# Filling TensorE's gaps in a graph attention layer: an earlier turn, a value product moved, rows normalised ahead

## The chip, the core and the metric

The kernel runs on one core of one Trainium2 chip. The metric is the device time of one execution in microseconds (us); lower is better. Before the change the median of three executions is 959.8 us (958.86 to 959.97).

A core has five engines that run side by side and wait for each other through semaphores. TensorE (PE) multiplies matrices and also transposes them, by a product with an identity; its results go to an accumulator memory called PSUM. VectorE (DVE), ScalarE (ACT) and GpSimd (POOL) do the elementwise work, and SyncE (SP) mostly issues DMA transfers between the device memory and the on-chip buffers. Every engine takes its own instructions in the order that was laid down when the kernel was built. That order is worked out by a scheduler from an estimate of durations; it follows the program as it is written where several instructions could go, but an instruction that the estimate holds to be ready may be put into a gap ahead of its place in the program.

## The reference

Two layers over the same 4096 nodes with 512 features, and one dense 4096 x 4096 matrix `adj`. Cut to what matters:

```python
# layer 0: attention inside each of 32 graphs of 128 nodes; b and edge_encoding are both adj
h = relu(layernorm(x))
query, key, value = h @ Wq.T + bq, h @ Wk.T + bk, h @ Wv.T + bv
a = where(mask, query @ key.T / sqrt(512), 0)
scores = (a + adj + adj) * where(mask, 1, -1e6)      # mask: same graph
x = x + (softmax(scores) * mask) @ value
# layer 1: 8 heads of 64; the attention's logits are s_i + t_j where adj > 0
h = relu(layernorm(x))
mx = einsum('nf,hfd->hnd', h, W)
attn = softmax(where(adj > 0, s_i + t_j, -inf))
x = x + concat_heads(attn @ mx)
```

In layer 0 only the 128 x 128 blocks on the diagonal enter the attention, but every entry of `adj` enters the softmax's sum. In layer 1 the term s_i is the same in a whole row and falls out of the softmax, so the kernel needs exp(t_j) only, and a 0/1 mask made of `adj`.

## The kernel before

The 4096 rows are 32 tiles of 128, and layer 0 takes two tiles (a pair, `G = 2`) at a time: 16 pairs. Query and key weights are multiplied together once ("fold"), so that scores are `(h M + c) h^T`. The products are in 32-bit floats.

First come the helpers that the change touches. `norm` is the layer norm: statistics on VectorE, the inverse root on GpSimd, the scaling on VectorE. `relu_T` turns a tile with four transpositions on TensorE and copies it out of PSUM on ScalarE, with the relu in the copy:

```python
    def norm(src, hn, of=None):
        mean, rstd = of or moments(src)
        nc.vector.tensor_scalar(hn, src, mean, rstd, ALU.subtract, ALU.mult)

    def relu_T(ps_pool, hn, dst):
        pt = ps_pool.tile([P, KC, P], F32, name="pt")
        for k in range(KC):
            nc.tensor.transpose(pt[:, k, :], hn[:, ts(k, P)], ident)
        nc.scalar.activation(dst, pt, AF.Relu)
```

The fold, cut to its product, which is made in four quarters `m`:

```python
    def fold(sb, tmp, work, ps_t, ps_p):
        wkT_sb = load_weight(tmp, wkT, "wkT_sb", KC, tag="lo")
        wqT_sb = load_weight(tmp, wqT, "wqT_sb", KC, tag="lo")
        # ... both turned back (L195), the biases' terms (L209) ...
        for m in range(KC):
            if m == 2:
                # ... u_sb and z_sb, the biases' terms spread over the partitions
            pp = ps_p.tile([P, D], F32, name="pp")
            for k in range(KC):
                nc.tensor.matmul(                                              # L231
                    pp, wq[:, k, ts(m, P)], wk[:, k, :], start=(k == 0), stop=(k == KC - 1)
                )
            nc.scalar.mul(m_sb[:, m, :], pp, SCALE)
        return m_sb, c_sb, u_sb, z_sb
```

Layer 0's parts for a pair, and for a row tile of layer 1 that is prepared while layer 0 still runs:

```python
            def normed1(i):                          # layer 1, row tile i
                row = sb2.tile([P, D], F32, name="row1")     # two buffers
                nc.sync.dma_start(row, x1_d[i])              # L392
                norm(row, row)
                hT = sb2.tile([P, KC, P], F32, name="hT1")
                relu_T(ps_t, row, hT)
                return hT

                def normed(g):
                    hT = sb.tile([P, KC, G * P], F32, name="hT")
                    r = sb.tile([P, G], F32, name="r", bufs=3)
                    hns = []
                    for t in range(G):
                        hn = sb.tile([P, D], F32, name="hn")  # two buffers
                        norm(xg[g][:, t, :], hn)
                        relu_T(ps_t, hn, hT[:, :, ts(t, P)])
                        hns.append(hn)
                    for t, hn in enumerate(hns):
                        # ... r = relu(hn) . u_sb + z_sb, on VectorE (L433) and GpSimd
                    return hT, r
```

`queries` is 16 matmuls for a pair (L445) with four copies on ScalarE to `gT` (L449); `values` is four products for a tile (L457) and an addition on VectorE; `scores` multiplies `gT` and `hT` (L503), adds twice the diagonal block of `adj` and takes the exponential on ScalarE; `turned` transposes the exponentials (L522) and has ScalarE copy them to `sT`; `attend` multiplies `sT` with the values (L530), adds the input on VectorE and stores the row as `x1_d`. `read` goes over the pair's rows of `adj`: VectorE makes the mask bytes of layer 1, and ScalarE takes the exponential of all entries for the sum (L480, `junk`), and the next loads of `adj` are issued.

The head and the loop over pairs:

```python
                m_sb, c_sb, u_sb, z_sb = fold(wp, lo, sb, ps_t, ps_p)
                load_pair(0)
                wv = load_weight(wp, wvT, "wv")
                # ... bv, seven loads of adj, load_pair(1) ...
                hT, r = normed(0)
                vs = [values(hT, t) for t in range(G)]
                # ... look: read of pair 0 ...
                gT = queries(hT)
                nhT, nr = normed(1)
                for g in range(NG):
                    # ... load_pair(g + 2) ...
                    def prepare_on(now):
                        if now:
                            i = len(ahead)
                            ahead.append(normed1(i))
                            if i:
                                prepare(i - 1, ahead[i - 1], part_tile(lo, i - 1))

                    s = scores(g, hT, gT, r, *look)
                    prepare_on(last)
                    if not last:
                        ngT = queries(nhT)
                    sT = turned(s)
                    prepare_on(3 <= g and g % 2)
                    nvs = []
                    for t in range(G):
                        look_on(t)                    # read of the next pair
                        attend(sT, vs[t], g, t)
                        prepare_on(last and t == 0)
                        if not last:
                            nvs.append(values(nhT, t))
                    # ... the next pair takes over ...
                    if g + 2 < NG:
                        nhT, nr = normed(g + 2)
```

`prepare` is layer 1's projection of one row tile (L259, 16 matmuls) with its exponentials. After the loop the remaining row tiles of layer 1 are prepared, and then the mask is multiplied with the prepared rows (L308), row tile by row tile.

Of the kernel before, what the change touches and what calls it, by code (L numbers as in the profile page):

```python
# [20 lines left out]
P = 128  # L21
# [32 lines left out]
def kernel(  # L54
# [53 lines left out]
    def load_adj(pool, k):  # L108

        a = pool.tile([P, NH], F32, name="a")  # L110
        nc.sync.dma_start(a, adj[ts(k // 2, P), ts(k % 2, NH)])
        return a
# [14 lines left out]
# [4 lines that stand above are left out]
# [19 lines left out]
    def load_weight(pool, src, name, pieces=1, **kw):  # L150
        t = pool.tile([P, KC, D], F32, name=name, **kw)
        n = KC // pieces
        for k in range(0, KC, n):
            nc.sync.dma_start(
                t[:, k : k + n], src[k * P : (k + n) * P].rearrange("(k p) m -> p k m", p=P)
            )
        return t
# [12 lines left out]
            )  # L170
        return w

    def fold(sb, tmp, work, ps_t, ps_p):


        wkT_sb = load_weight(tmp, wkT, "wkT_sb", KC, tag="lo")
        wqT_sb = load_weight(tmp, wqT, "wqT_sb", KC, tag="lo")
        def spread_bias(b):
            pp = ps_p.tile([P, D], F32, name="pp")
            for k in range(KC):  # L180
                nc.tensor.matmul(
                    pp[:, ts(k, P)], b[:, k : k + 1].to_broadcast([P, P]), ident,
                    start=True, stop=True,
                )
            row = work.tile([P, D], F32, name="b_row", tag="hn")
            nc.scalar.copy(row, pp)
            return row

        nat = []
        for n, wT in enumerate((wkT_sb, wqT_sb)):  # L190
            w = tmp.tile([P, KC, D], F32, name=f"w{n}", tag="lo")
            for k in range(KC):
                pt = ps_t.tile([P, KC, P], F32, name="pt")
                for m in range(KC):
                    nc.tensor.transpose(pt[:, m, :], wT[:, k, ts(m, P)], ident)  # L195
                nc.scalar.copy(w[:, :, ts(k, P)], pt)
                if n == 0 and k == 0:
                    rows = [spread_bias(b) for b in (bk_sb, bq_sb)]
            nat.append(w)
        wk, wq = nat  # L200
        m_sb = sb.tile([P, KC, D], F32, name="m_sb")
        c_sb = sb.tile([P, KC], F32, name="c_sb")
        u_col = sb.tile([P, KC], F32, name="u_col")
        u_sb = sb.tile([P, D], F32, name="u_sb")
        z_sb = sb.tile([P, 1], F32, name="z_sb")
        for dst, wT, row in ((u_col, wqT_sb, rows[0]), (c_sb, wkT_sb, rows[1])):
            for k in range(KC):
                wb = work.tile([P, D], BF16, name="wb", tag="hu", bufs=1)
                nc.vector.scalar_tensor_tensor(  # L209
                    wb, wT[:, k, :], SCALE, row, ALU.mult, ALU.mult, accum_out=dst[:, k : k + 1]  # L210
                )
        zk = sb.tile([P, KC], F32, name="zk")
        zp = sb.tile([P, 1], F32, name="zp")
        nc.vector.scalar_tensor_tensor(
            zk, bq_sb, SCALE, bk_sb, ALU.mult, ALU.mult, accum_out=zp
# [6 lines that stand above are left out]
                        pp[:, ts(k, P)], u_col[:, k : k + 1].to_broadcast([P, P]), ident,  # L222
                        start=True, stop=True,
                    )
                nc.scalar.copy(u_sb, pp)
                pp = ps_p.tile([P, D], F32, name="pp")
                nc.tensor.matmul(pp[:, :1], zp.to_broadcast([P, P]), one, start=True, stop=True)
                nc.scalar.copy(z_sb, pp[:, :1])
            pp = ps_p.tile([P, D], F32, name="pp")
            for k in range(KC):  # L230
                nc.tensor.matmul(  # L231
# [4 lines that stand above are left out]
# [136 lines left out]
    with ExitStack() as straight:  # L372
# [4 lines left out]
        with ExitStack() as prep:  # L377
# [9 lines left out]

            two = []

            def normed1(i):  # L390
                row = sb2.tile([P, D], F32, name="row1")
                nc.sync.dma_start(row, x1_d[i])  # L392
                norm(row, row)
                hT = sb2.tile([P, KC, P], F32, name="hT1")
                relu_T(ps_t, row, hT)
                return hT
# [17 lines left out]
            with (  # L414
# [2 lines left out]
                tc.tile_pool(name="sb0", bufs=2, side="right") as sb,  # L417
                tc.tile_pool(name="ps_s0", bufs=1, space=PSUM) as ps_s,
            ):
                def normed(g):  # L420


                    hT = sb.tile([P, KC, G * P], F32, name="hT")
                    r = sb.tile([P, G], F32, name="r", bufs=3)
                    hns = []
                    for t in range(G):
                        hn = sb.tile([P, D], F32, name="hn")
                        norm(xg[g][:, t, :], hn)
                        relu_T(ps_t, hn, hT[:, :, ts(t, P)])
                        hns.append(hn)  # L430
                    for t, hn in enumerate(hns):
                        hu = sb.tile([P, D], BF16, name="hu", bufs=1)
                        nc.vector.scalar_tensor_tensor(  # L433
                            hu, hn, 0.0, u_sb, ALU.max, ALU.mult, accum_out=r[:, t : t + 1]
                        )
                    nc.gpsimd.tensor_scalar(r, r, z_sb, None, ALU.add)
                    return hT, r

                def queries(hT):

# [96 lines left out]
                def load_pair(g):  # L537
                    xg[g] = sb.tile([P, G, D], F32, name="xg", bufs=3)
                    nc.sync.dma_start(
                        xg[g], x[g * G * P : (g + 1) * G * P, :].rearrange("(t p) d -> p t d", p=P)  # L540
                    )

                NG = NT // G
                xg, aa = {}, {}
                m_sb, c_sb, u_sb, z_sb = fold(wp, lo, sb, ps_t, ps_p)
                load_pair(0)
                wv = load_weight(wp, wvT, "wv")
                nc.scalar.dma_start(bv_sb, bv.to_broadcast([P, D]))
                for k in range(4):
                    aa[k] = load_adj(ap, k)  # L550
                load_pair(1)
                for k in range(4, AB):
                    aa[k] = load_adj(ap, k)
                hT, r = normed(0)
                vs = [values(hT, t) for t in range(G)]
                look = seen()
                for t in range(G):
                    look[2].append(read(t, look[0][:, t, :], look[1][t]))
                gT = queries(hT)
                nhT, nr = normed(1)  # L560
                ahead = []
                for g in range(NG):
                    last = g + 1 == NG
                    if g + 2 < NG:
                        load_pair(g + 2)
                    if g == 1:
                        w1x = load_w1(pool1, sb)
                    nlook = seen()

                    def look_on(t):  # L570
                        if not last:
                            i = G * (g + 1) + t
                            nlook[2].append(read(i, nlook[0][:, t, :], nlook[1][t]))

                    def prepare_on(now):
                        if now:
                            i = len(ahead)
                            ahead.append(normed1(i))
                            if i:
                                prepare(i - 1, ahead[i - 1], part_tile(lo, i - 1))  # L580

                    s = scores(g, hT, gT, r, *look)
                    prepare_on(last)
                    if not last:
                        ngT = queries(nhT)
                    sT = turned(s)
                    prepare_on(3 <= g and g % 2)
                    nvs = []
                    for t in range(G):
                        look_on(t)  # L590
                        attend(sT, vs[t], g, t)
                        prepare_on(last and t == 0)
                        if not last:
                            nvs.append(values(nhT, t))
                    if not last:
                        hT, r, gT, vs, look = nhT, nr, ngT, nvs, nlook
                    if g + 2 < NG:
                        nhT, nr = normed(g + 2)

# [477 lines left out]
```

## Time and profile before

| | before |
|---|---|
| median time | 959.8 us |
| span of the profiled execution | 956.0 us |
| TensorE busy / weight loads busy | 934.7 us / 810.8 us |
| VectorE busy | 465.0 us |
| ScalarE busy | 267.9 us |
| GpSimd busy | 179.9 us |
| aggregate products of layer 1 (L308, two groups) | 247.4 and 237.3 us |
| projection of layer 1 (L259) | 117.0 us |
| value products (L457) | 116.4 us |
| query products (L445) | 113.2 us |
| bytes moved by DMA | 156.63 MB, mean 164 GB/s |

All lines of the profile are of one profiled execution. A timeline row gives the start in us from the span's start, the duration in us, the engine, the line of the kernel, the operation with what it writes and reads, how many instructions are merged in the row, and in brackets how long the engine was idle before it and what ended that. "PE" is TensorE's matmuls and transpositions, "PEld" its weight loads, which overlap with them. The times of matmuls in the timeline overlap a little with their neighbours, because matmuls are pipelined and their ends are modelled; the chain of waits counts each only until the next begins. "MATMUL pt" are transpositions of rows, "pp" products.

Layer 0 fills the first 350 us or so, with TensorE, VectorE, ScalarE and the DMA engines all at work; the rest of layer 1's rows is prepared until about 460 us; from there to the end the aggregate products run one after another.

### The profile page before, as it was taken

The numbers are of one execution on the slowest core, as the hardware profiler recorded it, in microseconds if no ns is written. First come the engines' busy times: TensorE is split into PE (matmuls) and PEld (weight loads), VectorE is DVE, ScalarE is ACT, GpSimd is POOL, SyncE is SP. The second block draws the span as 40 slices with busy tenths as digits, with TensorE's granted clock in tenths as the row PEclk, the third lists the DMA queues.
The fourth block names the chain that finished last, engine by engine and source line by source line (L and its number), as shares of the span: only waits on it lengthen the run. The fifth ranks groups of instructions, "written<-read, shape, count | busy, mean of one in ns | idle before, by whom it ended". The sixth has DMA issues, their size and how long they took to land.

```text
span 956.0 us, 13142 instructions
## 1 busy us (share of the span) xinstructions
PE 934.7 (98%) x4987; PEld 810.8 (85%) x4987; DVE 465.0 (49%) x992; ACT 267.9 (28%) x539; POOL 179.9 (19%) x344
## 2 busy tenths in 40 slices
PE   8999999999999999999999999999999999999997
PEld 5676667776666777778999999999999999999997
DVE  4678877775775445674445242423324242423322
ACT  5776576666662224532000000000000000000000
POOL 2311213211211224655210100101010110101010
PEclk9999999999999999999999999999999999999999
DMA  9989889998985213575131312122231313222111
GB/s 343 417 344 390 332 312 364 348 367 322 367 349 199 78 34 110 165 198 133 56 85 49 88 50 84 51 82 72 61 89 45 89 50 83 57 77 85 48 45 36
DMA packets 61062, 156.63 MB, mean 164 GB/s; under 512 B 6722, under 2 KB 23490, under 8 KB 52290
## 3 DMA queue, kind: packets, MB, share of 16 engines
q1 hardware_dynamic: 51058, 138.70, 42.0%
q10 hardware_dynamic: 9936, 17.05, 4.8%
q8 instruction: 40, 0.66, 0.3%
q14 instruction: 28, 0.23, 0.1%
HBM read 117.97 MB, written 37.75 MB: 163 GB/s over the span
## 4 chain that ended last, share of the span: by engine, by line
PE 86%; DVE 4%; DMA 4%; ACT 3%; issue 1%; POOL 1%; SPq 0%; ACTq 0%; DVEq 0%
PE pg L308 50%; PE pp L457 12%; PE pp L445 10%; PE pp L259 5%; PE pp L530 3%; PE pss L503 3%; PE pt L136 1%; DMA row<-x_d 1%; DVE stats L118 1%; DMA a<-adj 1%; PE pl L308 1%; DVE blocks L623 1%; ACT rowm L698 1%; POOL rstd L124 1%; DMA mw<-a_d 1%
## 5 line engine op out<-in xcount | busy, mean ns | idle before, releaser
L308 PE MATMUL pg<-part,ata 128*128 128x348 f32 x1536 | 247.4, 322 | 0.6 <-DVE e L268 0.6
L308 PEld LDWEIGHTS pg<-part,ata 128*128 128x128 f32 x1536 | 245.0, 188 | 1.0 <-issue 1.0
L308 PE MATMUL pg<-part,atb 128*128 128x348 f32 x1472 | 237.3, 322 | 0.0
L308 PEld LDWEIGHTS pg<-part,atb 128*128 128x128 f32 x1472 | 235.0, 188 | 0.1
L321 ACT COPY tot<-pg 128x522 f32<-128x522 f32 x31 | 18.6, 599 | 455.9 <-PE pg L308 455.9
L480 ACT ACTIVATE junk<-a 128x2048 bf16<-128x2048 f32 (+15 forms) x92 | 124.5, 1353 | 49.9 <-DVE x L532 28.0
L259 PE MATMUL pp<-w1x,hT 128*128 128x256 f32 (+1 forms) x512 | 117.0, 384 | 2.0 <-DVE e L268 1.8
L457 PE MATMUL pp<-wv,hT 128*128 128x512 f32 x256 | 116.4, 598 | 0.0
L445 PE MATMUL pp<-hT,m_sb 128*128 128x256 f32 x512 | 113.2, 379 | 0.0
L259 PEld LDWEIGHTS pp<-w1x,hT 128*128 128x128 f32 x512 | 95.3, 190 | 19.3 <-issue 4.7
L296 DVE CAST atb<-at 128x4096 fp32r<-128x4096 fp8e4 x16 | 36.7, 2293 | 153.1 <-PE pg L308 153.1
L445 PEld LDWEIGHTS pp<-hT,m_sb 128*128 128x128 f32 x512 | 96.2, 190 | 12.8 <-issue 0.5
L296 DVE CAST ata<-at 128x4096 fp32r<-128x4096 fp8e4 (+1 forms) x17 | 37.3, 2196 | 141.8 <-PE pg L308 141.8
L457 PEld LDWEIGHTS pp<-wv,hT 128*128 128x128 f32 x256 | 49.2, 192 | 61.8 <-issue 61.8
L146 DVE TENSOR_SCALAR a<-a 128x512 fp8e4<-128x512 f32 x256 | 98.8, 466 | 1.6 <-DMA a_d<-a 1.4
L733 POOL COPY den_all<-tot 128x1 f32<-128x1 f32 x31 | 5.7, 184 | 367.9 <-DVE tot L322 355.9
L737 POOL TENSOR_TENSOR tot<-tot,row 128x512 f32<-128x512 f32 x31 | 39.9, 1286 | 61.9 <-DVE tot L327 57.8
L122 POOL TENSOR_SCALAR ve<-mv 128x1 f32<-128x1 f32 x64 | 16.3, 258 | 163.3 <-DVE mv L120 163.3
L243 POOL TENSOR_TENSOR part<-e,part 128x522 fp32r<-128x522 f32 x32 | 42.8, 1336 | 18.5 <-ACT part L240 18.4
L287 DVE STREAM_TRANSPOSE at<-mw 128x1024 f32<-128x1024 f32 x32 | 39.6, 1238 | 5.3 <-DMA mw<-a_d 5.3
L124 POOL TENSOR_TENSOR rstd<-ve,neghalf 128x1 f32<-128x1 f32 x64 | 38.5, 604 | 4.6
L461 DVE TENSOR_TENSOR v<-pp,bv_sb 128x512 f32<-128x512 f32 x32 | 22.0, 689 | 32.2 <-PE pp L457 32.2
(113 smaller groups left out, 691.0 us busy)
## 6 DMA issues: line engine op xcount, KB each, us to landing
a<-adj SPq DMA_DIRECT2D x64, 1024.0 KB, 12.8
a_d<-a SPq DMA_DIRECT2D x32, 512.0 KB, 10.1
mw<-a_d SPq DMA_DIRECT2D x128, 128.0 KB, 4.0
row<-x_d SPq DMA_DIRECT2D x41, 256.0 KB, 3.5
xg<-x SPq DMA_DIRECT2D x16, 512.0 KB, 4.6
x_d<-x ACTq DMA_DIRECT2D x32, 256.0 KB, 4.2
out<-tot ACTq DMA_DIRECT2D x31, 256.0 KB, 3.7
rowm<-x_d SPq DMA_DIRECT2D x16, 256.0 KB, 4.8
```

The costliest lines, as they stand in the source:

```text
L124: nc.gpsimd.tensor_tensor(rstd, ve, neghalf, ALU.pow)
L146: nc.vector.tensor_scalar(a8v[:, u], av[:, u], 0.0, None, ALU.is_gt, saturate=False)
L243: nc.gpsimd.tensor_sub(dst[:, :, 1, :], e3, dst[:, :, 0, :].bitcast(F32))
L259: nc.tensor.matmul(pm[g][:, :n], hT[:, k, :], w1x[:, k, g * HW : g * HW + n], start=(k == 0), stop=(k == KC - 1),)
L287: nc.vector.transpose(at8.rearrange("p c n b -> p (c n b)").bitcast(F32).rearrange("p (c u n) -> p c u n", c=NW, n=B), mw.rearrange("p u ( ...
L296: nc.vector.tensor_copy(at[:, c0 * BY : c1 * BY].rearrange("p (c b) q -> p c b q", b=BY), at8[:, c0:c1].rearrange("p c q b -> p c b q"),)
L308: nc.tensor.matmul(pg[:, : 2 * CW1], at[:, j, :], part(j)[:, c].rearrange("p s w -> p (s w)"), start=(j == 0), stop=(j == NT - 1),)
L445: nc.tensor.matmul(pp[:, : G * P], m_sb[:, k, ts(m, P)], hT[:, k, :], start=(k == 0), stop=(k == KC - 1),)
L457: nc.tensor.matmul(pp, hT[:, k, ts(t, P)], wv[:, k, :], start=(k == 0), stop=(k == KC - 1))
L480: nc.scalar.activation(junk[:, c0:c1], a[:, c0:c1], AF.Exp, scale=2.0 * NEG, accum_out=sums[:, n : n + 1],)
L503: nc.tensor.matmul(pss[:, t, :], gT[:, k, ts(t, P)], hT[:, k, ts(t, P)], start=(k == 0), stop=(k == KC - 1),)
L737: nc.gpsimd.tensor_add(num, num, row)
```

## The change

There are three parts. None changes what is computed.

- Pair 0 is turned within the fold, ahead of the last quarter of the weights' product, by a function that the fold calls at `m == 3`. For this `normed` is cut in two: `turned0` normalises and turns, `row_terms` makes `r`. The loads that used to follow the fold in the program are handed to it too and are written right after its own. The aim is that the value product of pair 0 finds its turned rows ready when the fold ends.
- In the loop, the next pair's first value product comes between the turned exponentials and the first attention instead of after it, so that the copy of `sT` has a product to hide behind.
- `normed1` is cut in two: `begin1` loads and normalises a row tile of layer 1, `turned1` turns it. A row is begun one turn ahead of the turn in which it is transposed (a turn is an odd pair from 3 on, and three times in the last pair), with its first load moved to pair 2, so that its transpositions have no load or normalisation to wait for.

The diff, with blank lines and unchanged stretches cut:

```diff
-    def fold(sb, tmp, work, ps_t, ps_p):
+    def fold(sb, tmp, work, ps_t, ps_p, loads, first):
         wkT_sb = load_weight(tmp, wkT, "wkT_sb", KC, tag="lo")
         wqT_sb = load_weight(tmp, wqT, "wqT_sb", KC, tag="lo")
+        loads()
@@ in the four quarters of the product
+            if m == 3:
+                first()
             pp = ps_p.tile([P, D], F32, name="pp")
@@
-            def normed1(i):
+            rows1 = []
+
+            def begin1():
                 row = sb2.tile([P, D], F32, name="row1")
-                nc.sync.dma_start(row, x1_d[i])
+                nc.sync.dma_start(row, x1_d[len(rows1)])
                 norm(row, row)
+                rows1.append(row)
+
+            def turned1(row):
                 hT = sb2.tile([P, KC, P], F32, name="hT1")
                 relu_T(ps_t, row, hT)
                 return hT
@@
-                def normed(g):
+                def turned0(g):
                     hT = sb.tile([P, KC, G * P], F32, name="hT")
-                    r = sb.tile([P, G], F32, name="r", bufs=3)
                     ...
+                    return hT, hns
+
+                def row_terms(hns):
+                    r = sb.tile([P, G], F32, name="r", bufs=3)
                     for t, hn in enumerate(hns):
                         ...
-                    return hT, r
+                    return r
@@
-                m_sb, c_sb, u_sb, z_sb = fold(wp, lo, sb, ps_t, ps_p)
-                load_pair(0)
-                wv = load_weight(wp, wvT, "wv")
-                ... (bv, adj, load_pair(1): the same lines)
-                hT, r = normed(0)
+                first = []
+
+                def loads():
+                    load_pair(0)
+                    first.append(load_weight(wp, wvT, "wv"))
+                    ... (bv, adj, load_pair(1): the same lines)
+
+                m_sb, c_sb, u_sb, z_sb = fold(
+                    wp, lo, sb, ps_t, ps_p, loads, lambda: first.extend(turned0(0))
+                )
+                wv, hT, hns = first
+                r = row_terms(hns)
@@
-                nhT, nr = normed(1)
+                nhT, hns = turned0(1)
+                nr = row_terms(hns)
@@ in the loop over pairs
-                            ahead.append(normed1(i))
+                            ahead.append(turned1(rows1[i]))
@@
                     prepare_on(last)
+                    if last:
+                        begin1()
                     if not last:
                         ngT = queries(nhT)
                     sT = turned(s)
                     prepare_on(3 <= g and g % 2)
+
+                    for _ in range({2: 1, NG - 2: 1, NG - 1: 0}.get(g, int(3 <= g and g % 2))):
+                        begin1()
                     nvs = []
                     for t in range(G):
                         look_on(t)
+                        if not last and t == 0:
+                            nvs.append(values(nhT, t))
                         attend(sT, vs[t], g, t)
                         prepare_on(last and t == 0)
-                        if not last:
+                        if not last and t:
                             nvs.append(values(nhT, t))
@@
-                        nhT, nr = normed(g + 2)
+                        nhT, hns = turned0(g + 2)
+                        nr = row_terms(hns)
```

More of the change, by code (lines that the diff above doesn't have):

```diff
@@ L544 @@
                 xg, aa = {}, {}
-                m_sb, c_sb, u_sb, z_sb = fold(wp, lo, sb, ps_t, ps_p)
-                load_pair(0)
-                wv = load_weight(wp, wvT, "wv")
[L548 to L553, printed above, removed]
-                hT, r = normed(0)
+                first = []
+                def loads():
+                    load_pair(0)
+                    first.append(load_weight(wp, wvT, "wv"))
+                    nc.scalar.dma_start(bv_sb, bv.to_broadcast([P, D]))
+                    for k in range(4):
+                        aa[k] = load_adj(ap, k)
+                    load_pair(1)
+                    for k in range(4, AB):
+                        aa[k] = load_adj(ap, k)
+                m_sb, c_sb, u_sb, z_sb = fold(
[3 more added lines that the diff above has]
+                r = row_terms(hns)
                 vs = [values(hT, t) for t in range(G)]
```

## The prediction, made before the changed kernel was run

> **What bounds the kernel now.** I read the page first, then the list of what TensorE waited for, then the timeline of TensorE alone through layer 0, and last the timelines of ScalarE and of the DMA issues around its three largest holes. The page's first part says which engine to look at:
>
> ```profile
> PE 934.7 (98%) x4987; PEld 810.8 (85%) x4987; DVE 465.0 (49%) x992; ACT 267.9 (28%) x539; POOL 179.9 (19%) x344
> ```
>
> TensorE is busy for 934.7 of 956.0 us. The change removes no matmul, so all it can return is idle TensorE time (21.3 us) and time in which matmuls run slower than they could. The wait list says how much of that has a cause with a name (columns: us in total, times, longest us):
>
> ```profile
> PE pt L195 <- DMA wkT_sb<-wkT: 3.8, 1, 3.8
> PE pt L136 <- DVE row L130: 2.6, 1, 2.6
> PE pp L530 <- ACT sT L524: 2.4, 4, 1.4
> PE pt L136 <- DVE hn L130: 2.0, 1, 2.0
> ```
>
> The first is the start of the program. The other three, 7.0 us together, are what the three parts aim at. The timeline shows each (start, duration, engine, what; in brackets the idle time before). First the head, TensorE and ScalarE:
>
> ```profile
> 27.22 1.04 PE L136 MATMUL pt<-ident,hn 128*128 128x128 f32 x8
> ...
> 28.38 1.08 ACT L137 ACTIVATE hT<-pt 128x512 f32<-128x512 f32 x2
> ...
> 30.27 0.33 PE L136 MATMUL pt<-ident,hn 128*128 128x128 f32 x1 [2.02 <-DVE hn L130]
> ...
> 30.44 7.04 PE L457 MATMUL pp<-wv,hT 128*128 128x512 f32 x16
> ```
>
> Pair 0 is turned at 27.22, after the whole weights' product. Its copy to hT ends only at 29.46, and one transposition of pair 1 has been put in the queue before the values, and waits for VectorE. TensorE idles from about 28.25 to 30.27. Next, pair 2 (L522 turns the exponentials, L530 is the attention):
>
> ```profile
> 91.63 0.38 PE L522 MATMUL pss<-ident,s 128*128 128x128 f32 x2
> 93.36 1.12 PE L530 MATMUL pp<-v,sT 128*128 128x512 f32 x2 [1.35 <-ACT sT L524]
> 94.32 3.60 PE L457 MATMUL pp<-wv,hT 128*128 128x512 f32 x8
> ```
>
> Attention needs sT, which ScalarE copies out of PSUM; the copy stood behind a 1.15 us and a 0.84 us exponential of the adjacency. The value product just after it (3.43 us in the chain) needs nothing of this. Last, pair 8:
>
> ```profile
> 213.31 1.04 PE L136 MATMUL pt<-ident,hn 128*128 128x128 f32 x8
> 216.95 0.44 PE L136 MATMUL pt<-ident,row 128*128 128x128 f32 x2 [2.60 <-DVE row L130]
> 217.22 1.34 PE L530 MATMUL pp<-v,sT 128*128 128x512 f32 x2
> 218.36 5.02 PE L457 MATMUL pp<-wv,hT 128*128 128x512 f32 x8
> ```
>
> A transposition of a layer 1 row waits for VectorE, and the value product after it takes 5.02 instead of 3.60 us. The chain of waits over this stretch names the row's DMA as the root, and the table by windows shows the clock that was granted (before the last two numbers):
>
> ```profile
> 203.59 10.84 DMA row<-x_d
> ...
> 214.45 0.70 DVE stats L118
> ```
>
> ```profile
> 210.00:220.00 10.00, 7.40 (x32) 5.01 (x31) 6.69 (x22) 6.70 (x13) 1.37 (x4) 0.89 1.02 423
> ```
>
> The row was issued at 203.59, in the middle of a burst of adjacency loads that starts when the old pair's input comes free (201.07), and landed 10.84 us later.
>
> **What the Trainium skill says.** "TensorE: Matmul & The Clock Gate", Part 1 (The HAM clock gate), says that about 3.4 us without work halves the clock and that the window runs freely. The trace agrees in part: after the hole at 213 to 217 the mean clock was 0.89, while after the shorter hole at 28 to 30 it stayed at 1.00. The same page, in its paragraph on engine queue depths, says that ScalarE and VectorE queues are strictly first in, first out; here ScalarE ran the last gT copy and then sT at 216.12 only after an exponential that had waited until 213.86 for its DMA, which agrees. "DMA: Bandwidth & Descriptors", Issuing engines are not separate DMA queues, lets one expect a small load to share the same 16 engines with the large ones; the row's 10.84 us beside a median of 4.8 us for its line agrees.
>
> **The change, part by part.** I take the distance from one pair's scores to the next pair's in the chain of waits, and compare it with the sum of the parts when nothing waits: scores 1.79, queries 6.91, turning the exponentials 0.22, attention twice 0.86, values twice 3.43, turning the next pair 0.87: 18.37 us. A pair that also prepares a layer 1 row has 3.51 for the projection and 0.43 for four transpositions: 22.31.
>
> Measured, pairs 1 to 13: 18.70, 20.00, 19.24, 18.90, 22.31, 18.71, 22.31, 23.11, 22.09, 18.70, 22.48, 18.70, 22.31. Pairs 5, 7, 9 and 13 lose nothing, because there the projection already stands between turning and attention (9 has two transpositions fewer). So the loss sits in these:
>
> Part B, a value product between turned exponentials and attention. Pairs 1, 6, 10 and 12 lose 0.33 each, with five transpositions as the filling, and pair 14 0.3 by the same sum without a next pair to turn: 1.6 together. Pair 2 loses 20.00 - 18.37 = 1.6; pair 3, with its 0.43 of row transpositions taken off, 0.4; pair 4 0.5; pair 11 0.2. Pair 0 loses 0.6 of wait and 0.3 of a slower first matmul: 0.9. In all 5.3. After the change 3.43 us of independent matmul lie there. The longest delay from the end of turning to sT is about 3.0 us, in pair 8 (213.4 to 216.5), so it just fits. Nothing is added; the first attention moves back 3.43, its result is stored that much later and read much later. I count 4 of 5.3, because the instruction order is laid out anew and some filling transpositions will move.
>
> Part C, rows one turn ahead. Pair 8 takes 23.11, against 18.37 plus 0.22 for two row transpositions: 4.5 lost, 2.6 of it the wait, 1.4 the value product at the lower clock, the rest at the attention. Loading and normalising the row in an odd pair for the next odd pair gives it some 40 us (two pairs) where 10.84 of landing and 2.5 of normalising (214.45 to 216.90) were needed. DMA bytes and VectorE work stay the same. But without the row wait, sT at 216.5 would still have stopped TensorE at pair 8: only B and C together bring 4.5. I count 3.5.
>
> Part A, pair 0 turned before the last quarter of the weights' product. Both normalised tiles are ready at 18.2 and 21.4, and the second last quarter ends near 23.7. The eight transpositions take 0.87 wherever they stand, so the values could start at 28.25 instead of 30.44: at most 2.2. The copy to hT must then pass a ScalarE that is 9.76 of 10 us busy from 20 to 30; if it falls behind the 1.91 us exponential that ends at 27.4, half is left. I count 1.5. Issuing the loads earlier in the program brings nothing: they are issued from 5.41 on already.
>
> Sum: 4 + 3.5 + 1.5 = 9.0 of at most 12.0. Off that I take about 0.7 for a wait that the new order makes somewhere: 959.8 - 8.3 = 951.5.
>
> **The rivals.** *DMA becomes the bound.* If adjacency tiles came at a fixed pace, TensorE would only run into a later sT: a faster head would be given back at pair 1 or 2, and the time would stay near 957. For it: the DMA share is about 1.0 from 10 to 60 us. Against it: the loads are issued in bursts that begin when the preceding pair's second attention has freed its input, so they move with TensorE; a pair moves 6.3 MB (four adjacency loads of 1024 KB, two mask stores and one input of 512 KB, two stores of 256 KB), some 15 us at the 420 GB/s seen in bursts, against 18.4 of matmuls; and between bursts the share falls (0.52 from 220 to 230). I give it 15%.
>
> *The new order makes a new wait.* Both holes of transpositions came from a filling instruction put ahead of one that was ready. With other gaps, others are placed, and a transposition can again stand before its row or pair has been normalised. One such miss with the clock drop costs 2 to 4.5 us: the time would be 954 to 957, two of them none gained. I give it 25%.
>
> *The layer's end turns over.* Row 8 can load only when row 6 has left its buffer, in the last pair. By the parts above it then has about 8.5 us until it is needed, for 3.5 of landing and 2.5 of normalising. It fits; a delay of the exponentials' end would cost 1 to 3 us. 10%.
>
> **Range and chances.** All that can be won is about 12 us, 1.3%; so faster by over 2% is out of reach (1%). To be slower by over 2% it would need 19 us of new waits, more than the whole kernel before has after its start (1%). The range is 947 (everything counted is won, and the trace's 12 us is a little short) to 957.5 (two of the three parts given back).
>
> **What would show it.** A: the transpositions of pair 0 stand between the third and fourth quarter of L231 and the value product starts near 28.3; wrong if it starts after 29.5. B: L457 follows L522 directly in the even pairs, and the wait for sT is gone from the list or under 0.5 us; the even pairs are 18.4 apart. C: no wait of TensorE for a row, and a granted clock of 1.00 from 200 to 250; the rows' DMA is issued two pairs before use. TensorE's busy time should fall by only the 1 to 3 us of slower matmuls, and idle time by 6 or more. The prediction is wrong if layer 1's first aggregate product, now at 460.46, does not start 7 to 10 us earlier, or if what layer 0 wins is lost between 350 and 460, where VectorE and ScalarE set the pace in places.

## The result

The changed kernel takes 947.1 us (median of 4, 946.73 to 947.57) where the kernel before takes 959.42 (median of 4): a ratio of 0.9875, 95% interval 0.9859 to 0.9891, or 12.3 us less. The prediction was 951.5 in a range of 947.0 to 957.5. The kernel is faster by less than 2%, as foretold, and the gain was half as large again as the 8.3 us counted: the time stands at the lower edge of the range, and one of the four executions (946.73) is below it.

The page's first part after the change, and then the whole list of what TensorE waited for (us in total, times, longest us):

```profile
PE 930.3 (98%) x4987; PEld 808.8 (86%) x4987; DVE 463.0 (49%) x992; ACT 267.2 (28%) x539; POOL 183.7 (19%) x344
```

```profile
PE pt L198 <- DMA wkT_sb<-wkT: 4.2, 2, 3.8
PE pp L264 <- DVE e L273: 1.8, 1, 1.8
PE pt L136 <- DVE rown L130: 1.8, 3, 0.9
PE pg L313 <- DVE e L273: 0.6, 1, 0.6
PE pp L236 <- ACT m_sb L239: 0.3, 1, 0.3
PE pp L470 <- ACT hT L137: 0.3, 1, 0.3
```

The span is 945.3 us against 956.0. TensorE's busy time is 4.4 us less and its idle time 15.0 instead of 21.3. The waits for a row and for sT are gone from the list; what is left before layer 1 is the start and twice 0.3 us in the head. (The lines of the kernel moved: 231 is now 236, 457 is 470, 522 is 535, 530 is 543.)

The timeline of TensorE in the changed kernel: the head, pair 2 and pair 8.

```profile
20.99 3.70 PE L236 MATMUL pp<-w,w 128*128 128x512 f32 x8 [0.34 <-ACT m_sb L239]
24.53 1.04 PE L136 MATMUL pt<-ident,hn 128*128 128x128 f32 x8
25.40 3.60 PE L236 MATMUL pp<-w,w 128*128 128x512 f32 x8
29.29 7.13 PE L470 MATMUL pp<-wv,hT 128*128 128x512 f32 x16 [0.29 <-ACT hT L137]
...
89.48 0.38 PE L535 MATMUL pss<-ident,s 128*128 128x128 f32 x2
89.70 3.60 PE L470 MATMUL pp<-wv,hT 128*128 128x512 f32 x8
93.14 1.88 PE L543 MATMUL pp<-v,sT 128*128 128x512 f32 x4
...
208.04 0.38 PE L535 MATMUL pss<-ident,s 128*128 128x128 f32 x2
208.26 3.60 PE L470 MATMUL pp<-wv,hT 128*128 128x512 f32 x8
212.01 1.98 PE L543 MATMUL pp<-v,sT 128*128 128x512 f32 x4
```

The reader sees the transpositions of pair 0 between two quarters of the weights' product, the value product directly behind the turned exponentials, and in pair 8 a short wait for sT, too short for the list: without it the attention would start at 211.69, not at 212.01.

The same distances as in the prediction, from one pair's scores to the next pair's, taken from TensorE's timelines (the sums of parts are 18.37 and 22.31; in pair 3, and wherever four row transpositions stand without a projection, 18.81; in pair 14, which has no next pair to turn, 17.50):

| pair | 0 | 1 | 2 | 3 | 4 | 5 | 6 | 7 | 8 | 9 | 10 | 11 | 12 | 13 | 14 |
|---|---|---|---|---|---|---|---|---|---|---|---|---|---|---|---|
| before | 19.24 | 18.70 | 19.99 | 19.25 | 18.90 | 22.31 | 18.70 | 22.32 | 23.10 | 22.10 | 18.70 | 22.47 | 18.70 | 22.32 | 18.37 |
| after | 18.37 | 18.37 | 18.38 | 18.81 | 18.37 | 22.32 | 18.37 | 22.32 | 18.78 | 22.32 | 18.37 | 22.32 | 18.37 | 22.37 | 17.50 |

Fourteen of fifteen pairs are at their sum within 0.1 us. The first scores start 0.95 us earlier (44.04 for 44.99), the last scores 10.78 earlier (339.38 for 350.16), layer 1's first aggregate 10.39 earlier (450.07 for 460.46). So nothing of importance is given back between 350 and 460. From 200 to 250 us the granted clock is 1.00. The profile shows 10.7 us of gain and the medians 12.3, because the profiled execution of the kernel before (957.75) was quicker than the four in the median (958.86 to 959.97).

### The profile page after: what moved, and what is told of

Its sections match the earlier page's. It is cut to its first block, busy times and chain, and to the rows that moved or that the text cites. A ratio compares the mean times of both kernels' runs of the same rounds, so it can differ in the third digit from the quotient of the medians.

```text
span 945.3 us, 13142 instructions
## 1 busy us (share of the span) xinstructions
PE 930.3 (98%) x4987; PEld 808.8 (86%) x4987; DVE 463.0 (49%) x992; ACT 267.2 (28%) x539; POOL 183.7 (19%) x344
## 4 chain that ended last, share of the span: by engine, by line
PE 87%; DMA 4%; DVE 3%; ACT 3%; POOL 1%; issue 1%; SPq 1%; ACTq 0%; DVEq 0%
PE pg L313 51%; PE pp L458 11%; PE pp L470 11%; PE pp L264 5%; PE pp L543 3%; PE pss L516 3%; DMA a<-adj 2%; PE pt L136 2%; ACT junk L493 1%; PE pl L313 1%; DVE blocks L652 1%; DVE stats L118 1%; ACT rowm L727 1%; DMA wkT_sb<-wkT 1%; POOL rstd L124 1%
## 5 line engine op out<-in xcount | busy, mean ns | idle before, releaser
L470 PE MATMUL pp<-wv,hT 128*128 128x512 f32 x256 | 115.0, 593 | 0.3 <-ACT hT L137 0.3
L146 DVE TENSOR_SCALAR a<-a 128x512 fp8e4<-128x512 f32 x256 | 96.9, 458 | 4.9 <-DMA a_d<-a 4.9
L137 ACT ACTIVATE hT<-pt 128x512 f32<-128x512 f32 x48 | 26.8, 594 | 48.1 <-PE pt L136 37.8
```

What stands on the lines that cost most here:

```text
L146: nc.vector.tensor_scalar(a8v[:, u], av[:, u], 0.0, None, ALU.is_gt, saturate=False)
L470: nc.tensor.matmul(pp, hT[:, k, ts(t, P)], wv[:, k, :], start=(k == 0), stop=(k == KC - 1))
```

## The experiments

Three runs take one part out of the change, three have one part alone, one repeats the changed kernel, and five go further. Each ratio is to the kernel before, run beside it on the same chip; there it took 956.8, 957.3 and 958.0 us (medians on three chips). "Below" is the ratio's distance from one times that median. The numbers in brackets behind a time are its range, behind a ratio its 95% interval.

### Without part A

```diff
-        loads()
-            if m == 3:
-                first()
+                m_sb, c_sb, u_sb, z_sb = fold(wp, lo, sb, ps_t, ps_p)
+                loads()
+                first.extend(turned0(0))
```

> Without part A (pair 0 turned after the whole weights' product, loads written after the fold), B and C kept. Theory: A is worth what the head of the trace shows, 1.2 to 1.7 us, and nothing of it is given back later: 948.3 to 948.8 beside 947.1 for the whole change; the value product of pair 0 starts about 30.4 again. Rival, the adjacency loads come at their own pace: TensorE runs into a later sT in pairs 0 to 2, and the time stays within 0.3 us of the whole change.

Measured: 949.27 us (947.76 to 951.22), ratio 0.992 (0.9905 to 0.9936). Its head, in TensorE's timeline, and the window from 30 to 40 us:

```profile
26.96 1.04 PE L136 MATMUL pt<-ident,hn 128*128 128x128 f32 x8
30.02 0.33 PE L136 MATMUL pt<-ident,hn 128*128 128x128 f32 x1 [2.02 <-DVE hn L130]
30.18 8.74 PE L466 MATMUL pp<-wv,hT 128*128 128x512 f32 x16
```

```profile
30.00:40.00 10.00, 9.98 (x23) 4.92 (x24) 6.25 (x17) 5.51 (x8) 2.37 (x4) 0.83 1.02 419
```

The hole of 2.02 us is the kernel before's, but the value product after it took 8.74 instead of 7.04 us, at a mean granted clock of 0.83 (the third number from the end). So the hole can cost the idle time and 1.7 us more. Three of the six executions took 947.76 to 948.43 us at a mean clock of 0.998 to 0.999 over the whole run, the other three 950.11 to 951.22 at 0.996 to 0.997, which fits a clock that drops after the hole in about half of them. The median of 949.27 is above the 948.3 to 948.8 expected, and 2.8 above that of the run without C (946.46, shown below), which was measured beside it. Nothing of A is given back later: the even pairs keep 18.37. The rival of a fixed DMA pace falls.

### Without part B

```diff
-                        if not last and t == 0:
-                            nvs.append(values(nhT, t))
                         attend(sT, vs[t], g, t)
-                        if not last and t:
+                        if not last:
                             nvs.append(values(nhT, t))
```

> Without part B (attention before the value product again), A and C kept. Theory: the waits for sT come back in the pairs without a projection, 5.3 us, and pair 8 stops for sT instead of for the row, some 2 us with no drop of the clock: 953.5 to 955. Rival, the row's wait and the clock drop in pair 8 were the main loss and the small gaps hardly count: 950 to 951.5.

Measured: 951.9 us (951.12 to 952.96), ratio 0.9951 (0.9937 to 0.9965). The waits for sT are back (2.8 us in the list, 4 times), and from the first to the last scores it is 301.07 us where the changed kernel has 295.34: up to there B is worth 5.7 us with the two others present. From the first scores to layer 1's first aggregate it is 5.5 (406.0 us against 411.5), because without B five transpositions of a layer 1 row stand in pair 14 that B moves behind the last scores. The total lies between the two outcomes stated. Pair 8 took 18.70 and did not stop for sT; pair 6, which now holds four row transpositions, took 19.78 and stopped there.

### Without part C

```diff
-                    if last:
-                        begin1()
-                    for _ in range({2: 1, NG - 2: 1, NG - 1: 0}.get(g, int(3 <= g and g % 2))):
-                        begin1()
+                            begin1()
                             ahead.append(turned1(rows1[i]))
```

> Without part C (a row is loaded, normalised and turned in one go), A and B kept. Theory of the prediction: pair 8 needs both B and C, so 3.5 to 4.5 us are lost again: 950.6 to 951.6. Rival: the row's transpositions stood in pair 8 only because there was a gap to fill; with the value product in that gap they go back to the odd pairs, where the row has long landed, and C is worth under 1 us: 947.1 to 948.

Measured: 946.46 us (945.57 to 946.69), ratio 0.9889 (0.9873 to 0.9905), just below the time of the rival. This decides against the prediction. Its pairs 8 and 9 in TensorE's timeline:

```profile
206.84 0.38 PE L535 MATMUL pss<-ident,s 128*128 128x128 f32 x2
207.05 3.60 PE L470 MATMUL pp<-wv,hT 128*128 128x512 f32 x8
210.49 1.88 PE L543 MATMUL pp<-v,sT 128*128 128x512 f32 x4
212.21 3.60 PE L470 MATMUL pp<-wv,hT 128*128 128x512 f32 x8
...
225.21 0.38 PE L535 MATMUL pss<-ident,s 128*128 128x128 f32 x2
225.43 0.60 PE L136 MATMUL pt<-ident,row 128*128 128x128 f32 x4
225.86 3.67 PE L264 MATMUL pp<-w1x,hT 128*128 128x264 f32 x16
```

No transposition of a row stands in pair 8 any more. All four are in pair 9, at 225.43, where the program has them, and the row, although loaded and normalised in one go, had been normalised at 214.79. Before the change the scheduler had moved two of them forward into the gap between L522 and L530. With B no such gap is left, none is moved, and C has nothing left to mend.

### VectorE's order in the preparation of layer 1

The wait list names VectorE three times after 350 us. There a row took 5.05 us (rows 10 to 14) for 3.94 of TensorE, in a ring: VectorE turned the far row, made statistics, normalised after GpSimd's part, ScalarE applied the relu, and VectorE stood idle for that relu before the next turn. The turn of row far - 1 moves behind the statistics, which don't need it:

```diff
-                    if MIXED < far <= NT:
-                        turn(far - 1)
                     # ... move, low ...
                     if far < NT:
                         of[far] = moments(rows[far])
                     if near < MIXED:
                         of[near] = moments(rows[near])
+                    if MIXED < far <= NT:
+                        turn(far - 1)
```

> The changed kernel, and between 350 and 450 us VectorE turns the far row after the statistics of the next rows instead of before them, so that it does not stand idle for ScalarE's relu. Theory: that stretch is paced by a ring of VectorE, GpSimd and ScalarE, 5.05 us a row for rows 10 to 14 and 3.74 for later ones, against 3.95 and 3.51 of TensorE; breaking the ring gives 4 to 7 us: 940 to 943. Rival: VectorE's own work or the part's split on GpSimd paces it: 946 to 947.1.

Measured: 940.45 us (938.66 to 941.45), ratio 0.983 (0.9816 to 0.9845), 6.0 us below the run without C beside it. The timeline of TensorE and VectorE (start, duration in us) around the same turn, in the changed kernel and then in this one:

```profile
368.08 0.66 PE L136 MATMUL pt<-ident,rown 128*128 128x128 f32 x4 [0.89 <-DVE rown L130]
...
369.18 0.71 DVE L652 STREAM_TRANSPOSE blocks<-rowm 128x512 f32<-128x512 f32 x1 [0.69 <-ACT rowm L727]
```

```profile
368.17 0.69 DVE L118 BATCH_NORM_STATS2 stats<-rowm 128x6 f32<-128x512 f32 x1
368.89 0.18 DVE L120 BATCH_NORM_AGGREGATE mv<-stats 128x2 f32<-128x6 f32 x1
368.99 0.66 DVE L118 BATCH_NORM_STATS2 stats<-rown 128x6 f32<-128x512 f32 x1
369.29 0.60 PE L136 MATMUL pt<-ident,rown 128*128 128x128 f32 x4
369.69 0.18 DVE L120 BATCH_NORM_AGGREGATE mv<-stats 128x2 f32<-128x6 f32 x1
369.79 0.68 DVE L652 STREAM_TRANSPOSE blocks<-rowm 128x512 f32<-128x512 f32 x1
```

In the changed kernel the turn has 0.69 us of idle time before it, here none, and TensorE's transpositions of rows follow each other at 3.94 us instead of 5.05. From the last scores to the first aggregate it takes 103.75 us instead of 110.69: 6.9 us, with the same instructions. After the head TensorE has one named wait left, of 0.6 us.

### The changed kernel again, and the parts alone

> The changed kernel once more, beside its single parts on the same chip. It should be 11 to 12.5 us below the kernel before of these runs, and spread by about 1 us, while the kernel before spreads by about 4, because its two holes sometimes drop the clock and sometimes don't.

Measured: 946.11 us (945.62 to 946.88), ratio 0.988 (0.9866 to 0.9894); the kernel before spread from 955.57 to 960.33. Its spread goes with the clock: of 16 executions the three slowest (959.37 to 960.33) had a mean clock of 0.995 to 0.996, the fastest 1.000, the others 0.997 to 0.999. Which hole lost the clock in each is not shown, as only one execution of the kernel before has a trace.

Part A alone has the fold's part of the diff, the other two parts as before the change:

> Part A alone: pair 0 turned within the fold. Theory: 1.5 us when the clock holds in the kernel before and 3.3 us when it drops after the hole at 28 to 30 us, 1.5 to 3 below the kernel before in the median, with no spread from the head. Rival, the waits for sT in pairs 0 to 2 take it back: 0 to 0.7 below.

Measured: 955.36 us (953.93 to 956.19), ratio 0.9976 (0.9967 to 0.9985), 2.3 us below. Pairs 0 to 7 are those of the kernel before, and pair 8 has its hole and the slow matmuls again:

```profile
214.66 0.44 PE L136 MATMUL pt<-ident,row 128*128 128x128 f32 x2 [2.46 <-DVE row L130]
214.93 1.02 PE L543 MATMUL pp<-v,sT 128*128 128x512 f32 x2
215.79 5.29 PE L470 MATMUL pp<-wv,hT 128*128 128x512 f32 x8
```

Part B alone has only the value product moved:

> Part B alone: a value product ahead of the attention. New theory: it wins its own 5.3 us and pair 8's 4.5 as well, because no row is turned in a gap that is no longer there: 8.5 to 10 below the kernel before. The prediction's theory, that pair 8 needs C too: 5 to 6 below.

Measured: 948.61 us (948.0 to 949.13), ratio 0.991 (0.9895 to 0.9924), 8.6 us below. Pair 8 takes 18.37, so B alone wins both the gaps for sT and pair 8. The head is as before the change, and in this execution the same hole let the clock be:

```profile
29.53 0.33 PE L136 MATMUL pt<-ident,hn 128*128 128x128 f32 x1 [2.02 <-DVE hn L130]
29.69 7.04 PE L466 MATMUL pp<-wv,hT 128*128 128x512 f32 x16
```

Part C alone has only the rows begun a turn ahead:

> Part C alone: rows begun one turn ahead. The row's wait in pair 8 is gone; either pair 8 then stops for sT instead (theory of the prediction), and the whole is 1 to 2.5 below the kernel before, or it takes its even pace of 18.7, and the whole is 3.5 to 4.5 below.

Measured: 953.99 us (median of 6), ratio 0.9961 (0.9949 to 0.9974), 3.7 us below. One of the six took 3374 us; it is not in the ratio, its cause is not known, and the other five lie between 952.81 and 955.47. Pair 8 takes 18.70, without a stop. A row's four transpositions fill pair 6 instead, and pairs 6 and 10 now wait for sT. Pair 6:

```profile
171.93 1.04 PE L136 MATMUL pt<-ident,hn 128*128 128x128 f32 x8
172.80 0.60 PE L136 MATMUL pt<-ident,row 128*128 128x128 f32 x4
174.11 1.13 PE L539 MATMUL pp<-v,sT 128*128 128x512 f32 x2 [0.71 <-ACT sT L533]
```

So C is a cure for pair 8 of its own, a second one, though it moves part of the loss to pairs 6 and 10 (19.79 and 19.34, against 18.70 each before). The three parts alone add up to 14.6, and together they give 11.5 beside them. The 3.1 between is about what C wins alone: it is won once, by B or by C.

### C once more, on the better version

> The changed kernel with VectorE's turn of the far row placed after the statistics, once more, as the partner of the next run: 16 to 17 us below the kernel before.

Measured: 939.49 us (938.53 to 940.15), ratio 0.9803 (0.9785 to 0.982).

> The same without part C. If C is worth nothing once B is there, the two agree within 0.5 us; if it still covers a late row or keeps ScalarE's order better, this one is 0.6 to 1.5 us slower. The prediction's theory (C needed in pair 8): 3.5 to 4.5 us slower, which the run without C has already spoken against.

Measured: 939.05 us (938.72 to 939.88), ratio 0.9804 (0.9787 to 0.9821). With B present C is worth nothing that these runs can tell from zero. This version, with A, B and VectorE's turn moved, and a row loaded and normalised in its own turn, is the simpler of the two fastest.

### Both value products ahead of both attentions

```diff
                         if not last and t == 0:
-                            nvs.append(values(nhT, t))
+                            nvs = [values(nhT, v) for v in range(G)]
                         attend(sT, vs[t], g, t)
-                        if not last and t:
-                            nvs.append(values(nhT, t))
```

> The changed kernel with both value products of the next pair ahead of the two attentions. If the adjacency loads follow the pair's second attention, as the issues showed, then they and the copy of sT that stands behind them move back by 3.43 us along with it: the wait for sT in pair 8 (0.3 to 0.6 us) stays or is covered, and the time is within 1 us of the changed kernel's. Rival, more to hide behind is simply better: 0.5 us faster, no wait for sT. Second rival, DMA comes too late for the masks and the reads: 2 us or more slower.

Measured: 948.34 us (947.9 to 949.97), ratio 0.99 (0.9884 to 0.9917), some 2 us slower than the changed kernel was (0.988), and 2.4 slower than the next run, measured beside it. No wait for sT is left, but there is a new one. Pair 10 in TensorE's timeline:

```profile
239.72 1.04 PE L136 MATMUL pt<-ident,hn 128*128 128x128 f32 x8
240.59 1.95 PE L516 MATMUL pss<-hT,gT 128*128 128x128 f32 x16
243.19 7.17 PE L458 MATMUL pp<-hT,m_sb 128*128 128x256 f32 x32 [0.66 <-ACT hT L137]
```

The queries wait for the copy of the turned pair (1.5 us in the list, 3 times). I expected neither this wait nor its size; of the three outcomes stated, none names it. ScalarE's timeline shows what that copy stands behind, here in pair 2, where it comes late in the same way (ACTq is ScalarE issuing a transfer):

```profile
79.66 1.05 ACTq L548 DMA_DIRECT2D x_d<-x  x2
80.76 1.09 ACT L137 ACTIVATE hT<-pt 128x512 f32<-128x512 f32 x2 [5.57 <-DVE x L545]
```

ScalarE issues the stores of the pair's rows ahead of the copy, and these wait for VectorE's addition after the second attention. In the changed kernel a value product lies between that attention and the transpositions; here there is none. The wait list has this wait of ScalarE 5 times, 13.3 us together, and in the changed kernel not at all.

### Five adjacency buffers instead of seven

```diff
-AB = 7
+AB = 5
```

> The changed kernel with five adjacency buffers instead of seven. If TensorE stays the bound only because the loads run far enough ahead, waits for sT come back in several pairs and the time rises by 5 to 20 us; if DMA has the slack that 6.3 MB a pair in 18.4 us suggests, it rises by less than 2.

Measured: 945.96 us (945.49 to 946.97), ratio 0.9874 (0.9853 to 0.9895), the changed kernel's own. Every pair takes its sum here, pair 8 too (18.37), with two buffers fewer to load ahead: DMA does not bound layer 0 in the changed kernel.

## Why the prediction was right, and where it was short

*What bounds.* Right in the main: TensorE's idle time fell by 6.3 us (6 or more foretold). But its busy time fell by 4.4, where 1 to 3 of slower matmuls were foretold. Of these, 1.4 is the value products (116.4 us before, 115.0 after), which is pair 8's slow one. Most of the rest lies in the attention products (34.0 us before, 30.3 after; the times of groups overlap and do not add up exactly). Waits as short as the 0.33 us of pairs 1, 6, 10 and 12 do not show as idle in TensorE's timeline, where the modelled ends of matmuls cover them; that they make up that rest is my reading, and no run separates it. The first aggregate starts 10.39 us earlier, beyond the 7 to 10 foretold.

*Part A.* The mechanism and the obstacle were as predicted: the copy to hT fell behind the 1.91 us exponential, as ScalarE's timeline shows, and TensorE waited 0.29 us for it.

```profile
26.26 1.91 ACT L493 ACTIVATE junk<-a 128x2048 bf16<-128x2048 f32 x1
...
28.17 0.58 ACT L239 ACTIVATE m_sb<-pp 128x512 f32<-128x512 f32 x1
28.65 1.07 ACT L137 ACTIVATE hT<-pt 128x512 f32<-128x512 f32 x2
```

The value product started at 29.29, not near 28.3: the weights' product itself began 0.53 us later, and TensorE waited 0.34 us within it and 0.29 behind it. From the start of that product to the values it is 16.68 us instead of 18.36: 1.7, near the 1.5 counted. Alone it measured 2.3 (1.4 to 3.2), which doesn't exclude 1.7. But the term left out that the old hole can cost the clock too, as the run without A shows: I had read from one profile that the clock stayed.

*Part B.* This term was mis-sized. Counted were 4 us of a possible 5.3; with A and C present the trace shows 5.5 up to the first aggregate, and alone it measured 8.6 (7.3 to 10.1). The deduction for a new order was not needed: with a product in the gap, the scheduler put no filling there, and every even pair but pair 8 came to its sum.

*Part C.* The step that failed is "only B and C together bring 4.5". B alone brings it (pair 8 at 18.37 instead of 23.10), because the row's early transpositions were a filling of the gap that B closes, and C alone brings pair 8 to 18.70. The 3.5 counted for C are 3.7 (2.5 to 4.9) alone and nothing beside B. That the sum did not suffer from it is luck: pair 8 was counted once, under the wrong part. What made the sum short were the discounts on B and C (2.3 us of 9.8), the 0.7 for a new wait, and, as far as it dropped, the clock in the head. The lead of the loads was also less than foretold: in the changed kernel the loads of rows 0 to 2 were issued 12 us before their transpositions and those of rows 3 to 5 26 to 30 us, not two pairs (some 40).

*The limit of B.* "It just fits" held to 0.4 us: pair 8 took 18.78, since sT was copied only at 211.59 to 211.95, 3.7 us after the turning, behind 3.43 us of product. When the same kernel ran again it took 18.99.

*The rivals.* DMA as the bound fell by its own test. New waits by a new order stayed small in layer 0: 0.3 us for hT in the head, which was foretold, and 0.3 for sT in pair 8. The end of the layer turned over without a loss: the last pair's transpositions follow each other with no wait.

## What to carry to other kernels

A stop at a small instruction that a scheduler moved into a gap is a symptom of the gap. Look first at what opened it: independent work of the same engine, long enough, put there by the program, removed here both the gap and the misplaced instruction, and made a second cure for the latter superfluous. And when a change of several parts is judged, take each part out and run each alone: here the parts alone add up to more than the whole.

## What the runs showed of the hardware

The same hole of 2.02 us in TensorE before the same 16 matmuls left them at 7.04 us in three profiles (the kernel before, B alone, C alone) and made them 8.74 in a fourth (without A), at a mean clock of 0.83 over 10 us; after a hole of about 2.5 us the product of 8 took 5.02 and 5.29 instead of 3.60. In the three profiles in which a hole cost the clock, it dropped 0.9 to 1.4 us after the hole had ended, and TensorE was granted half of it for 3.4 us each time (31.0 to 34.4 us without A, 217.8 to 221.2 in the kernel before, 216.1 to 219.5 with A alone): 1.7 us of matmuls, as much as 8.74 has over 7.04. "TensorE: Matmul & The Clock Gate" of the Trainium skill, Part 1, tells of about 3.4 us without work, in a window that runs freely; here holes of 2.0 us were enough, but not each time. Transpositions stand on both sides of each hole, and whether they count as work for the clock no run separates. One profile doesn't show what such a hole costs.
